# Layer 1's operands between two layers: half the rows transposed by VectorE and moved through DRAM, in a hand-made order

## The chip, the core and the metric

The program runs on one core of one Trainium2 chip. A core has five engines that run side by side and wait for one another on semaphores: TensorE (PE in the profile; its weight loads are PEld), VectorE (DVE), ScalarE (ACT), GpSimd (POOL) and SyncE (SP), which here only issues transfers. The metric is the device time of one execution in microseconds (us), the median of several runs. Positions "at 363.78" are us from the start of the profiled span.

## What is computed

Two layers of attention over 4096 nodes with 512 features; `x` is 4096 x 512 and `adj` 4096 x 4096, both float32. Cut to what matters:

```python
# layer 0: attention inside 32 graphs of 128 nodes each
h = relu(layernorm(x))
x = x + graph_attention(h, adj, adj, ptr, Wq, bq, Wk, bk, Wv, bv)

# layer 1: graph attention over the whole graph, 8 heads of 64
h   = relu(layernorm(x))
mx  = einsum('nf,hfd->hnd', h, W)
t_j = einsum('hnd,hd->hn', mx, a_dst)      # (s_i cancels in the softmax over j)
attn = softmax(where(adj > 0, s_i + t_j, -inf))
x = x + concat_heads(einsum('hij,hjd->hid', attn, mx))
```

In layer 1 the weight of neighbour `j` depends on `j` alone, so the kernel computes `e_j = exp(t_j)` once, multiplies the row `mx_j` by it, and then sums these rows over the neighbours with a 0/1 mask: numerator and denominator come out of one matmul with the mask as the weights. A layer norm of all rows of layer 0's result, a product with `W`, and the scaled rows ("parts") of all 32 row tiles have to stand in SBUF before the first of those sums can end.

## The kernel before

A tile is 128 rows; there are 32 tiles. The steps that the change touches, with cuts marked by `# ...`:

```python
def norm(src, hn):                       # layer norm of a tile
    stats = small.tile([P, 6], F32, name="stats")
    nc.vector.bn_stats(stats, src)                                   # L114
    mv = small.tile([P, 2], F32, name="mv")
    nc.vector.bn_aggr(mv, stats)                                     # L116
    ve = small.tile([P, 1], F32, name="ve")
    nc.gpsimd.tensor_scalar(ve, mv[:, 1:2], EPS, None, ALU.add)      # L118
    rstd = small.tile([P, 1], F32, name="rstd")
    nc.gpsimd.tensor_tensor(rstd, ve, neghalf, ALU.pow)              # L120
    nc.vector.tensor_scalar(hn, src, mv[:, 0:1], rstd, ALU.subtract, ALU.mult)  # L121

def relu_T(ps_pool, hn, dst):            # 4 transposes by TensorE, relu on the way out
    pt = ps_pool.tile([P, KC, P], F32, name="pt")
    for k in range(KC):
        nc.tensor.transpose(pt[:, k, :], hn[:, ts(k, P)], ident)     # L127
    nc.scalar.activation(dst, pt, AF.Relu)                           # L128

def project1(ps_m, hT, w1x):             # product with W, 16 matmuls in the profile
    pm = [ps_m.tile([P, D], F32, name="pp") for _ in range(2)]
    for g, n in ((1, HW + H), (0, HW)):
        for k in range(KC):
            nc.tensor.matmul(pm[g][:, :n], hT[:, k, :], w1x[:, k, g * HW : g * HW + n],
                             start=(k == 0), stop=(k == KC - 1))     # L243
    return pm

def weigh(e, pm):                        # rows times exp(t), two instructions
    for g in (1, 0):
        nc.vector.tensor_tensor(e[:, ts(g, HW)]..., pm[g]..., e[:, ES + ...]..., ALU.mult)  # L252

def split(e, dst):                       # a number as the sum of two fp32r numbers
    nc.scalar.copy(dst[:, :, 0, :], e3)                              # L230
    nc.gpsimd.tensor_sub(dst[:, :, 1, :], e3, dst[:, :, 0, :].bitcast(F32))  # L231

def load_mask(sb, i):                    # 0/1 bytes from DRAM, transposed, cast
    mw = sb.tile([P, P // B, N // BY // (P // B)], F32, name="mw", bufs=1)
    # ... four transfers mw <- a_d (L265)
    nc.vector.transpose(at8..., mw...)                               # L270, 128 x 1024
    at = sb.tile([P, NT, P], F32R, name="at")
    nc.vector.tensor_copy(at..., at8...)                             # L277, 128 x 4096
    return at

def aggregate(sb, ps_g, i, part):        # 32 x 3 matmuls for one tile of the output
    at = load_mask(sb, i)
    pg = ps_g.tile([P, CB, 512], F32, name="pg")
    for j in range(NT):
        for c in range(CB):
            product(pg[:, c], at, part, j, c)                        # L284
    # ...
```

Layer 0 runs first. Behind its last groups, tiles 0 to 8 of layer 1 are begun. Then comes the stretch between the layers, and after it the sums:

```python
def normed1(i):
    row = sb2.tile([P, D], F32, name="row1")
    nc.sync.dma_start(row, x1_d[i])      # layer 0's result, read back from DRAM
    norm(row, row)
    hT = sb2.tile([P, KC, P], F32, name="hT1")
    relu_T(ps_t, row, hT)
    return hT

def prepare(i, hT, part):
    pm = project1(ps_p, hT, w1x)         # ps_p has 4 buffers, a tile takes 2
    e = sb2.tile([P, EW], F32, name="e")
    nc.gpsimd.memset(e[:, EC:], 1.0)
    nc.scalar.activation(e[:, ES:EC], pm[1][:, HW : HW + H], AF.Exp) # L379
    nc.gpsimd.tensor_copy(e_all[:, i, :], e[:, ES:EC])               # L380
    weigh(e, pm)
    split(e, part)
    parts.append(part)

n = len(ahead)                           # 9: tiles 0 to 8 are begun
nhT = ahead[-1]
for i in range(n - 1, NT):
    hT = nhT
    if i + 1 < NT:
        nhT = normed1(i + 1)
    prepare(i, hT, part_tile(lo if i < LO else hi, i))

# ... hold(n, src, bound, op): two DVE instructions that check a range of values

for i in range(NT - 1):
    row = sb3.tile([P, D], F32, name="row3", bufs=1)
    nc.sync.dma_start(row, x1_d[i])
    tot = aggregate(sb3, ps_g, i, lambda j: parts[j])
    # ... divide by the denominator, add row, store
    if i == 1:
        graphs_are_tiles(sb3)            # checks on ptr, small DVE instructions
        hold(0, rs_all, 1.0 / S_MAX, ALU.is_ge)
        # ... three more
```

The order in which an engine gets its instructions is set by a scheduler when the program is built; it may put instructions of the sums (the first masks, the checks) between those of the stretch before. A branch for inputs that break the assumptions ("general") follows and is not taken here.

Of the kernel before, what the change touches and what calls it, by code (L numbers as in the profile page):

```python
# [9 lines left out]
F32 = mybir.dt.float32  # L10
# [10 lines left out]
P = 128  # L21
# [4 lines left out]
H = 8  # L26
# [15 lines left out]
SCALE = float(D) ** -0.5  # L42
BIG_T = 40.0
AB = 7
LO = 8
E_MIN, E_MAX = 4.3e-18, 2.3e17
S_MIN, S_MAX = 1e-15, 1e30
# [4 lines left out]
def kernel(  # L52
# [28 lines left out]

    a_d = dram.tile([NT, P, N // BY], F32, name="a_d")
    x1_d = dram.tile([NT, P, D], F32, name="x1_d")

    ident = const.tile([P, P], F32, name="ident")
# [20 lines left out]
        return a  # L108


    def norm(src, hn):

        stats = small.tile([P, 6], F32, name="stats")
        nc.vector.bn_stats(stats, src)  # L114
# [3 lines that stand above are left out]
        nc.gpsimd.tensor_scalar(ve, mv[:, 1:2], EPS, None, ALU.add)  # L118
        rstd = small.tile([P, 1], F32, name="rstd")
        nc.gpsimd.tensor_tensor(rstd, ve, neghalf, ALU.pow)  # L120
        nc.vector.tensor_scalar(hn, src, mv[:, 0:1], rstd, ALU.subtract, ALU.mult)  # L121

    def relu_T(ps_pool, hn, dst):

# [5 lines that stand above are left out]
    def mask_bytes(a8, a, h):  # L130

        half = ts(h, NW // 2)
        a8v = a8.rearrange("p (u c q b) -> p u c b q", c=NW, q=B, b=BY)[:, :, half]
        av = a.rearrange("p (c b u q) -> p u c b q", c=NW // 2, b=BY, q=B)
        for u in range(P // B):
            nc.vector.tensor_scalar(  # L136
                a8v[:, u], av[:, u], 0.0, None, ALU.is_gt, saturate=False
            )
# [94 lines left out]
    def load_row(pool, i):  # L233
        row = pool.tile([P, D], F32, name="row1")
        nc.sync.dma_start(row, x1_d[ds(i, 1)].rearrange("o p d -> (o p) d"))
        return row

    def project1(ps_m, hT, w1x):
# [4 lines that stand above are left out]
                nc.tensor.matmul(  # L243
                    pm[g][:, :n], hT[:, k, :], w1x[:, k, g * HW : g * HW + n],
                    start=(k == 0), stop=(k == KC - 1),
                )
        return pm

    def weigh(e, pm):

        for g in (1, 0):
            nc.vector.tensor_tensor(  # L252
                e[:, ts(g, HW)].rearrange("p (h d) -> p h d", d=HD),
                pm[g][:, :HW].rearrange("p (h d) -> p h d", d=HD),
                e[:, ES + g * H // 2 : ES + (g + 1) * H // 2, None].to_broadcast([P, H // 2, HD]),
                ALU.mult,
            )
# [48 lines left out]
    def graphs_are_tiles(sb):  # L306


        ptr_i = sb.tile([1, NPTR], I32, name="ptr_i", bufs=1)
        nc.sync.dma_start(ptr_i, ptr)  # L310
        ptr_f = sb.tile([1, NPTR], F32, name="ptr_f", bufs=1)
        nc.vector.tensor_copy(ptr_f, ptr_i)
        ends_i = sb.tile([1, NT, 2], I32, name="ends_i", bufs=1)
        nc.gpsimd.iota(ends_i, pattern=[[P, NT], [P - 1, 2]], base=0, channel_multiplier=0)
        ends = sb.tile([1, NT, 2], F32, name="ends", bufs=1)
        nc.vector.tensor_copy(ends, ends_i)
        ge = sb.tile([1, NT, 2], F32, name="ge", bufs=1)
        for t0 in range(0, NT, 4):
            cmp = sb.tile([1, 8, NPTR], F32, name="cmp", bufs=1)
            nc.vector.tensor_tensor(  # L320
                cmp,
                ends[:, t0 : t0 + 4].rearrange("p t e -> p (t e)")[:, :, None].to_broadcast(
                    [1, 8, NPTR]
                ),
                ptr_f[:, None, :].to_broadcast([1, 8, NPTR]),
                ALU.is_ge,
            )
            nc.vector.tensor_reduce(
                ge[:, t0 : t0 + 4].rearrange("p t e -> p (t e)"), cmp, AX.X, ALU.add
            )  # L330
        same = sb.tile([1, NT], F32, name="same", bufs=1)
        nc.vector.tensor_tensor(same, ge[:, :, 0], ge[:, :, 1], ALU.is_equal)
        later = sb.tile([1, NT - 1], F32, name="later", bufs=1)
        nc.vector.tensor_tensor(later, ge[:, 1:, 0], ge[:, : NT - 1, 1], ALU.is_gt)
        good = sb.tile([1, 2], F32, name="good", bufs=1)
        nc.vector.tensor_reduce(good[:, 0:1], same, AX.X, ALU.min)
        nc.vector.tensor_reduce(good[:, 1:2], later, AX.X, ALU.min)
        nc.vector.tensor_tensor(held[0:1, 6:7], good[:, 0:1], good[:, 1:2], ALU.mult)
# [8 lines left out]
    w1x = None  # L347
    parts = []
    with ExitStack() as straight:
        pool1 = straight.enter_context(tc.tile_pool(name="l1", bufs=1))  # L350
        sb2 = straight.enter_context(tc.tile_pool(name="sb2", bufs=2))
        lo = straight.enter_context(tc.tile_pool(name="lo", bufs=LO // 2))

        with ExitStack() as prep:
            ps_t = prep.enter_context(tc.tile_pool(name="ps_t0", bufs=3, space=PSUM))
            ps_p = prep.enter_context(tc.tile_pool(name="ps_p0", bufs=4, space=PSUM))

            def part_tile(pool, j):
                if j >= LO:
                    return pool.tile([P, CB, 2, CW1], F32R, name=f"part{j}")  # L360
                if j % 2 == 0:
                    two.append(pool.tile([P, 2, CB, 2, CW1], F32R, name=f"part{j}", tag="lo"))
                return two[-1][:, j % 2]
# [3 lines left out]
# [5 lines that stand above are left out]
                relu_T(ps_t, row, hT)  # L372
                return hT

            def prepare(i, hT, part):
                pm = project1(ps_p, hT, w1x)
                e = sb2.tile([P, EW], F32, name="e")
                nc.gpsimd.memset(e[:, EC:], 1.0)
                nc.scalar.activation(e[:, ES:EC], pm[1][:, HW : HW + H], AF.Exp)  # L379
                nc.gpsimd.tensor_copy(e_all[:, i, :], e[:, ES:EC])  # L380
                weigh(e, pm)
                split(e, part)
                parts.append(part)

            with (
                tc.tile_pool(name="w0", bufs=1, side="right") as wp,
                tc.tile_pool(name="adj0", bufs=AB, side="right") as ap,
                tc.tile_pool(name="sb0", bufs=2, side="right") as sb,
                tc.tile_pool(name="ps_s0", bufs=1, space=PSUM) as ps_s,
            ):  # L390
# [178 lines left out]
                        nhT, nr = normed(g + 2)  # L569


            hi = straight.enter_context(
                tc.tile_pool(name="hi", bufs=1, reuse_waits="tile")
            )
            n = len(ahead)
            nhT = ahead[-1]
            for i in range(n - 1, NT):
                hT = nhT
                if i + 1 < NT:
                    nhT = normed1(i + 1)  # L580
                prepare(i, hT, part_tile(lo if i < LO else hi, i))

# [81 lines left out]
    with tc.If(bad > 0, label="general"):  # L666
# [131 lines left out]
        with (  # L798
# [60 lines left out]
            with tc.For_i(0, n_levels, 1):  # L859
                with (  # L860
                    tc.tile_pool(name="sb4", bufs=2) as sb,
                    tc.tile_pool(name="ps_m4", bufs=2, space=PSUM) as ps_m,
                    tc.For_i(0, NT, 1) as i,
                ):
                    hT = sb.tile([P, KC, P], F32, name="hT1")
                    row = load_row(sb, i)
                    norm(row, row)
                    relu_T(ps_t, row, hT)
                    pm = project1(ps_m, hT, w1x)
                    te = small.tile([P, H], F32, name="te")  # L870
                    nc.vector.tensor_tensor(te, pm[1][:, HW : HW + H], shift, ALU.subtract)
                    nc.vector.tensor_scalar(te, te, 0.0, None, ALU.min)
                    e = sb.tile([P, EW], F32, name="e")
                    nc.gpsimd.memset(e[:, EC:], 1.0)
                    nc.scalar.activation(e[:, ES:EC], te, AF.Exp)
                    weigh(e, pm)
                    split(e, parts_e[:, ds(i, 1)].rearrange("p o c s w -> p (o c) s w"))
                with (
                    tc.tile_pool(name="sb5", bufs=1) as sb,
                    tc.tile_pool(name="ps_g5", bufs=1, space=PSUM) as ps_g,  # L880
# [62 lines left out]
```

## Time and profile before

| | |
|---|---|
| time, median of 3 | 964.26 us (963.89 to 967.47) |
| span of the profiled run | 961.1 us |
| TensorE busy | 937.3 us, 98% |
| its weight loads busy | 817.2 us, 85% |
| VectorE, ScalarE, GpSimd busy | 48%, 27%, 19% |
| granted TensorE clock | 0.999 |
| sums of layer 1 (L284, group `pg`) | 479.6 us busy, 3008 matmuls |

How to read it: an engine's busy time is the sum of its instructions; the part of the span that is missing from TensorE's is its idle time. Layer 0 takes the time to about 350, the stretch between the layers goes to about 466, and the sums take the rest. The profile also gives, for any stretch, the busy time of each engine, for each wait who released it, and the instructions in order of time.

### The profile page before, as it was taken

How to read it: one execution, taken by the hardware profiler on the slowest of the kernel's cores; microseconds unless marked ns; L12 is line 12 of the kernel's file. 1: busy time of each engine (PE TensorE's matmuls, PEld its weight loads, DVE VectorE, ACT ScalarE, POOL GpSimd, SP SyncE). 2: the span in 40 equal slices, each digit the busy share in tenths (PEclk: the TensorE clock that was granted, in tenths of full speed). 3: DMA queues.
4: the chain of work that ended last, by engine and by line, in shares of the span. 5: the costliest groups of instructions: out<-in, count | busy, mean ns of one | idle time of the engine just before them, and what ended most of it. 6: DMA issues, size and time to landing. Idle time of an engine off the chain costs nothing.

```text
span 961.1 us, 13194 instructions
## 1 busy us (share of the span) xinstructions
PE 937.3 (98%) x5051; PEld 817.2 (85%) x5051; DVE 460.7 (48%) x983; ACT 260.7 (27%) x507; POOL 185.0 (19%) x344
## 2 busy tenths in 40 slices
PE   8999999989999998899999999999999999999997
PEld 5676677766677776788899999999999999999997
DVE  4678777776766348655142332424233242423322
ACT  5766676666762222333100000000000000000000
POOL 2221213222122115555110101001010100101010
PEclk9999999999999999999999999999999999999999
DMA  9999889898884124222012213132231212122111
GB/s 347 419 349 389 314 324 368 351 369 343 343 335 158 34 87 122 77 66 55 1 54 80 85 49 88 49 83 54 79 82 50 88 50 83 52 80 81 51 45 35
DMA packets 58180, 148.22 MB, mean 154 GB/s; under 512 B 6402, under 2 KB 23170, under 8 KB 49922
## 3 DMA queue, kind: packets, MB, share of 16 engines
q1 hardware_dynamic: 48178, 130.31, 39.0%
q10 hardware_dynamic: 9936, 17.05, 4.7%
q8 instruction: 40, 0.66, 0.3%
q14 instruction: 26, 0.21, 0.1%
HBM read 113.77 MB, written 33.55 MB: 153 GB/s over the span
## 4 chain that ended last, share of the span: by engine, by line
PE 89%; DVE 4%; DMA 2%; POOL 2%; ACT 2%; issue 1%; SPq 0%; ACTq 0%; DVEq 0%; POOLq 0%
PE pg L284 50%; PE pp L428 11%; PE pp L416 10%; PE pp L243 9%; PE pp L501 3%; PE pss L474 3%; PE pt L127 2%; DMA row<-x_d 1%; PE pl L284 1%; POOL part L231 1%; DMA xg<-x 1%; DVE a L136 1%; DVE row L121 1%; ACT junk L451 1%; POOL rstd L120 0%
## 5 line engine op out<-in xcount | busy, mean ns | idle before, releaser
L284 PE MATMUL pg<-part,at 128*128 128x348 f32 x3008 | 479.6, 322 | 1.2 <-DVE e L252 1.2
L284 PEld LDWEIGHTS pg<-part,at 128*128 128x128 f32 x3008 | 479.1, 188 | 1.6 <-issue 1.5
L277 DVE CAST at<-at 128x4096 fp32r<-128x4096 fp8e4 x32 | 74.0, 2313 | 312.2 <-PE pg L284 312.2
L298 ACT COPY tot<-pg 128x522 f32<-128x522 f32 x31 | 18.5, 598 | 455.8 <-PE pg L284 455.8
L451 ACT ACTIVATE junk<-a 128x2048 bf16<-128x2048 f32 (+15 forms) x92 | 124.4, 1353 | 47.1 <-DVE x L503 25.0
L243 PE MATMUL pp<-w1x,hT 128*128 128x256 f32 (+1 forms) x512 | 117.3, 383 | 0.0
L428 PE MATMUL pp<-wv,hT 128*128 128x512 f32 x256 | 114.9, 592 | 0.0
L416 PE MATMUL pp<-hT,m_sb 128*128 128x256 f32 x512 | 113.2, 379 | 0.0
L416 PEld LDWEIGHTS pp<-hT,m_sb 128*128 128x128 f32 x512 | 96.2, 190 | 12.8 <-issue 0.5
L243 PEld LDWEIGHTS pp<-w1x,hT 128*128 128x128 f32 x512 | 94.9, 190 | 13.3
L428 PEld LDWEIGHTS pp<-wv,hT 128*128 128x128 f32 x256 | 48.6, 190 | 60.7 <-issue 60.7
L136 DVE TENSOR_SCALAR a<-a 128x512 fp8e4<-128x512 f32 x256 | 98.1, 460 | 1.8 <-DMA a_d<-a 1.8
L609 POOL COPY den_all<-tot 128x1 f32<-128x1 f32 x31 | 5.7, 184 | 369.2 <-DVE tot L299 369.2
L128 ACT ACTIVATE hT<-pt 128x512 f32<-128x512 f32 x64 | 36.9, 597 | 67.7 <-PE pt L127 67.6
L613 POOL TENSOR_TENSOR tot<-tot,row 128x512 f32<-128x512 f32 x31 | 39.9, 1288 | 61.8 <-DVE tot L304 61.8
L231 POOL TENSOR_TENSOR part<-e,part 128x522 fp32r<-128x522 f32 x32 | 42.2, 1318 | 43.1 <-ACT part L230 35.5
L118 POOL TENSOR_SCALAR ve<-mv 128x1 f32<-128x1 f32 x64 | 18.6, 294 | 150.9 <-DVE mv L116 150.8
L252 DVE TENSOR_TENSOR e<-pp,e 128x256 f32<-128x256 f32 x64 | 26.4, 415 | 29.3 <-ACT e L379 26.0
L270 DVE STREAM_TRANSPOSE at<-mw 128x1024 f32<-128x1024 f32 x32 | 39.6, 1236 | 0.0
L120 POOL TENSOR_TENSOR rstd<-ve,neghalf 128x1 f32<-128x1 f32 x64 | 38.4, 602 | 4.4
L432 DVE TENSOR_TENSOR v<-pp,bv_sb 128x512 f32<-128x512 f32 x32 | 22.0, 688 | 33.9 <-PE pp L428 33.9
L420 ACT ACTIVATE gT<-pp,c_sb 128x256 f32<-128x256 f32 x64 | 29.7, 467 | 28.7 <-PE pp L416 28.3
(101 smaller groups left out, 608.0 us busy)
## 6 DMA issues: line engine op xcount, KB each, us to landing
a<-adj SPq DMA_DIRECT2D x64, 1024.0 KB, 12.9
a_d<-a SPq DMA_DIRECT2D x32, 512.0 KB, 10.2
row<-x_d SPq DMA_DIRECT2D x64, 256.0 KB, 3.4
mw<-a_d SPq DMA_DIRECT2D x128, 128.0 KB, 4.0
xg<-x SPq DMA_DIRECT2D x16, 512.0 KB, 4.6
x_d<-x ACTq DMA_DIRECT2D x32, 256.0 KB, 4.2
out<-tot ACTq DMA_DIRECT2D x31, 256.0 KB, 3.8
wkT_sb<-wkT SPq DMA_DIRECT2D x4, 256.0 KB, 5.0
```

Of the source, the lines that this page charges most:

```text
L120: nc.gpsimd.tensor_tensor(rstd, ve, neghalf, ALU.pow)
L128: nc.scalar.activation(dst, pt, AF.Relu)
L136: nc.vector.tensor_scalar(a8v[:, u], av[:, u], 0.0, None, ALU.is_gt, saturate=False)
L231: nc.gpsimd.tensor_sub(dst[:, :, 1, :], e3, dst[:, :, 0, :].bitcast(F32))
L243: nc.tensor.matmul(pm[g][:, :n], hT[:, k, :], w1x[:, k, g * HW : g * HW + n], start=(k == 0), stop=(k == KC - 1),)
L270: nc.vector.transpose(at8.rearrange("p c n b -> p (c n b)").bitcast(F32).rearrange("p (c u n) -> p c u n", c=NW, n=B), mw.rearrange("p u ( ...
L277: nc.vector.tensor_copy(at.rearrange("p (c b) q -> p c b q", b=BY), at8.rearrange("p c q b -> p c b q"))
L284: nc.tensor.matmul(pg[:, : 2 * CW1], at[:, j, :], part(j)[:, c].rearrange("p s w -> p (s w)"), start=(j == 0), stop=(j == NT - 1),)
L416: nc.tensor.matmul(pp[:, : G * P], m_sb[:, k, ts(m, P)], hT[:, k, :], start=(k == 0), stop=(k == KC - 1),)
L428: nc.tensor.matmul(pp, hT[:, k, ts(t, P)], wv[:, k, :], start=(k == 0), stop=(k == KC - 1))
L451: nc.scalar.activation(junk[:, c0:c1], a[:, c0:c1], AF.Exp, scale=2.0 * NEG, accum_out=sums[:, n : n + 1],)
L613: nc.gpsimd.tensor_add(num, num, row)
```

## The change

Tiles 16 to 31 of layer 1 no longer go through TensorE's transposes. VectorE normalises the rows, ScalarE applies the relu, VectorE transposes 32 x 32 blocks, and four such tiles (a "block" of 1 MB) are stored to a DRAM tensor and loaded again so that the blocks land in the places of a whole transpose. The rows within a group of four tiles come out in another order; the mask's bytes of the second half of the columns are put into the same order, so that the sum is the same. Tiles 9 to 15 stay with TensorE. VectorE, ScalarE, GpSimd and SyncE keep the order in which the loop is written, 8 tiles ahead for the new kind of tile and 2 tiles ahead for the old kind. The pools of the stretch move to the other side of SBUF and end with it; the small `ptr` load shares a buffer with `row3`.

```diff
+MIXED = NT // 2
+AHEAD = 8
+    hT_d = dram.tile([NW, P, P // B, KC * P], F32, name="hT_d")
-    def norm(src, hn):
+    def moments(src):                       # the first four instructions of norm
...
+        return mv[:, 0:1], rstd
+    def norm(src, hn, of=None):
+        mean, rstd = of or moments(src)
+        nc.vector.tensor_scalar(hn, src, mean, rstd, ALU.subtract, ALU.mult)
...
-        av = a.rearrange("p (c b u q) -> p u c b q", c=NW // 2, b=BY, q=B)
+        order = ("p (c b u q) -> p u c b q", "p (c u b q) -> p u c b q")[h]
+        av = a.rearrange(order, c=NW // 2, b=BY, q=B)
...
-        ptr_i = sb.tile([1, NPTR], I32, name="ptr_i", bufs=1)
+        ptr_i = sb.tile([1, NPTR], I32, name="ptr_i", tag="row3", bufs=1)
...
-        pool1 = straight.enter_context(tc.tile_pool(name="l1", bufs=1))
-        sb2 = straight.enter_context(tc.tile_pool(name="sb2", bufs=2))
+            pool1 = prep.enter_context(tc.tile_pool(name="l1", bufs=1, side="right"))
+            sb2 = prep.enter_context(tc.tile_pool(name="sb2", bufs=2, side="right"))
...
-            for i in range(n - 1, NT):
-                hT = nhT
-                if i + 1 < NT:
-                    nhT = normed1(i + 1)
-                prepare(i, hT, part_tile(lo if i < LO else hi, i))
+            def load(i):
+                if i < NT:
+                    name, bufs = ("rowm", 5) if i >= MIXED else ("rown", 3)
+                    rows[i] = sb4.tile([P, D], F32, name=name, bufs=bufs)
+                    nc.sync.dma_start(rows[i], x1_d[i])
+            def turn(i):
+                c, b = divmod(i, BY)
+                if b == 0:
+                    blocks[c] = sb4.tile([P, P // B, KC, BY, B], F32, name="blocks")
+                nc.vector.transpose(
+                    blocks[c][:, :, :, b], rows[i].rearrange("p (k q f) -> p q k f", k=KC, f=B)
+                )
+                if b == BY - 1:
+                    nc.sync.dma_start(hT_d[c], blocks[c].rearrange("p q k b r -> p q (k b r)"))
+            def move(c):
+                hT = sb5.tile([P, P // B, KC, P], F32, name="hT4")
+                for q in range(P // B):
+                    nc.sync.dma_start(
+                        hT[ts(q, B)].rearrange("p u k m -> p u (k m)"),
+                        hT_d[c, :, q].rearrange("(u f) w -> f u w", f=B),
+                    )
+                for u in range(BY):
+                    hTs[c * BY + u] = hT[:, u]
+            with tc.manual_schedule(engines={E.DVE, E.Activation, E.Pool, E.SP}):
+                n = len(ahead) - 1                                  # 8
+                hTs[n] = ahead[n]
+                before = None
+                for i in (1, 2):
+                    load(n + i)
+                for i in range(MIXED, n + AHEAD + 2):
+                    load(i)
+                norm(rows[n + 1], rows[n + 1])
+                for i in range(n, NT):
+                    far, near = i + AHEAD, i + 2
+                    near_in = near < MIXED
+                    far_in = MIXED <= far < NT
+                    if near + 1 < MIXED:
+                        load(near + 1)
+                    load(far + 2)
+                    if MIXED <= far - 1 < NT:
+                        turn(far - 1)
+                    if (far - 2) % BY == BY - 1 and MIXED <= far - 2 < NT:
+                        move((far - 2) // BY)
+                    if far_in:
+                        of[far] = moments(rows[far])
+                    if near_in:
+                        of[near] = moments(rows[near])
+                    if i + 1 < MIXED:
+                        hTs[i + 1] = sb2.tile([P, KC, P], F32, name="hT1")
+                        relu_T(ps_t, rows[i + 1], hTs[i + 1])
+                    pm = project1(ps_p, hTs[i], w1x)
+                    if before:
+                        finish(*before)                             # weigh, split of tile i - 1
+                    if near_in:
+                        norm(rows[near], rows[near], of[near])
+                    if far_in:
+                        norm(rows[far], rows[far], of[far])
+                    before = (weights(i, pm), pm, part_tile(lo if i < LO else hi, i))
+                    if far_in:
+                        nc.scalar.activation(rows[far], rows[far], AF.Relu)
+                finish(*before)
```

`weights` and `finish` are the two halves of `prepare`. The rest of the diff is in the branch that is not taken.

## The prediction

> **What bounds the kernel now.** The first view is the page: the span and TensorE's busy share.
>
> ```profile
> span 961.1 us, 13194 instructions
> PE 937.3 (98%) x5051; PEld 817.2 (85%) x5051; DVE 460.7 (48%) x983; ACT 260.7 (27%) x507; POOL 185.0 (19%) x344
> ```
>
> TensorE is the bound: all its idle time together is 961.1 - 937.3 = 23.8 us. A change can win only by taking work from TensorE or by closing some of these gaps. The second view is busy time by stretch (columns: length, then busy us of each engine):
>
> ```profile
> 356.00:404.00 48.00, 41.83 (x203) 34.23 (x202) 38.98 (x79) 13.02 (x29) 25.98 (x49) 1.00 0.34 98
> 404.00:457.00 53.00, 53.00 (x270) 46.07 (x269) 29.34 (x66) 16.95 (x40) 30.31 (x68) 1.00 0.23 61
> 457.00:466.00 9.00, 7.83 (x39) 6.58 (x37) 3.46 (x9) 2.53 (x6) 2.82 (x5) 1.00 0.00 0
> ```
>
> Between the layers TensorE has 48.00 - 41.83 = 6.17 us of gaps while VectorE is loaded (38.98 of 48), then none for 53 us, then 1.17 us at the handover to the sums. The third view, TensorE's waits, says who ends them: mainly VectorE's normalised rows.
>
> ```profile
> PE pt L127 <- DVE row L121: 8.7, 5, 3.0
> PE pg L284 <- DVE e L252: 1.2, 1, 1.2
> ```
>
> The fourth, the chain in order of time, gives the steady tile: 3.51 us of product and 0.44 us of transposes, with nothing between.
>
> ```profile
> 437.69 3.51 PE pp L243 x16
> 441.20 0.44 PE pt L127 x4
> 441.63 3.51 PE pp L243 x16
> ```
>
> [...] a row normalisation at 375.39 took 1.44 us in place of 0.55 while GpSimd's subtraction (L231, from 375.32, 1.23 us) ran. [...]The page's row loads of 256 KB land in 3.4 us and pairs of 512 KB in 4.6[...].
>
> **Part 1: removed from TensorE.** 16 tiles x 0.44 us = 7.0 us of transposes, all on the path. ScalarE's copy out of PSUM (L128, 597 ns) goes too, and a relu of about the same size comes instead.
>
> **Part 2: the 6.2 us of gaps now.** They come because the scheduler put three masks (L270 1.24 + L277 2.3 us each) and the small ptr checks between the norms. By the built program's order these now all stand after the stretch. So these gaps go, if VectorE's new work doesn't make others.
>
> **Part 3: VectorE's new loop.** While both kinds of tile are in work (tiles 8 to 13) one turn of the loop is, in order, with start-to-start times as the trace has them where VectorE is packed: transpose 0.6 (half of L270's 1.24), twice stats and aggregate 0.83, two products with e 0.75, a wait of 0.25 (in the steady timeline a norm starts 1.0 us after its aggregate has ended, which is GpSimd's L118 and L120; the products hide 0.75 of it), two norms 0.5 each. That is 4.3 us. Then the last norm feeds ScalarE's relu and the relu feeds the next turn's first transpose: 0.1 + 0.6 + 0.1 = 0.8 us in which VectorE has nothing to do. 5.1 us a turn, against TensorE's 3.95. Walking the first turns from tile 8's product, at about 362.9 (363.78 now, less the 0.4 and 0.5 of gaps before it): VectorE is ahead by about one turn, so TensorE first waits at tile 11, 0.5 us, and then 1.25 or 1.3 at tiles 12, 13 and 14: 4.3 us together. With the far kind alone (tiles 14 to 23) a turn is 0.6 + 0.83 + 0.75 + 0.25 + 0.5 + 0.8 = 3.75 to 3.85 against 3.51: TensorE has only 2 x 2 PSUM buffers and follows, 8 x 0.33 = 2.6 us. After tile 23 VectorE has only the products and TensorE runs at 3.51.
>
> **Part 4: the trip through DRAM.** Four tiles make a store of 1 MB and four loads of 256 KB. The only 1 MB transfers of this kind that land while not queued by their own kind took 6.8 and 7.5 us; the loads need four issues at 0.45 us, and the last should land in some 4.5 us (the mask quarters of 128 KB on 32 partitions took 4.0). About 13 us from the block's last transpose to the product. The walk gives 16 us for the first block, 13.2 for the second and third, and 11.8 for the last, whose lead shrinks because TensorE no longer waits for VectorE. I count 1.3 us for the last and nothing for the others.
>
> **Part 5: the handover.** The built program has the first mask's transpose after the last product of VectorE's loop and after the range checks. The order now is shown by the timeline: checks in front of the last L252, the sums right after it, with their mask long ready.
>
> ```profile
> 463.60 0.29 DVE L595 TENSOR_SCALAR ok<-e_all 128x256 f32<-128x256 f32 x1 [0.16 <-POOL e_all L380]
> 463.93 0.42 DVE L596 TENSOR_REDUCE held<-ok 128x1 f32<-128x256 f32 x1
> 464.38 0.29 DVE L595 TENSOR_SCALAR ok<-e_all 128x256 f32<-128x256 f32 x1
> 464.71 0.42 DVE L596 TENSOR_REDUCE held<-ok 128x1 f32<-128x256 f32 x1
> 465.04 0.41 DVE L252 TENSOR_TENSOR e<-pp,e 128x256 f32<-128x256 f32 x1
> 465.60 20.63 PE L284 MATMUL pg<-part,at 128*128 128x348 f32 x128 [1.17 <-DVE e L252]
> ```
>
> After the change TensorE has to wait for: the last L252, 0.45; nine small checks, about 2.3 (the four of e_all above take 1.5); L270 1.2; L277 2.3; a start of 0.1. That is 6.4 us, against 1.17 now.
>
> **The sum.** From 362.9: 24 products x 3.51 = 84.2; 6 transposes left x 0.44 = 2.6; VectorE's turns 4.3 + 2.6; the last block 1.3; the handover 6.4. The sums start at 464.3, against 465.60 now: 1.3 us earlier. The 496 us after that hold the same matmuls in the same order; the ptr checks that move there (eight pairs of 0.83 us) fit in a tile's 15.5 us. Layer 0's matmuls keep their order. 964.26 - 1.3 = 963.0.
>
> **The rivals.** (a) *VectorE doesn't bind.* If the order of the loop leaves VectorE ahead, the 6.9 us of part 3 are gone, and the time is about 956. For it: far rows are taken 8 tiles ahead, and only the near norms and the PSUM buffers tie the two engines. Against it: the relu between two instructions of the same in-order engine, with nothing of VectorE's placed between. (b) *The DRAM trip binds.* If store and loads take 16 us in place of 13, three blocks stall 3 us each: about 971. For it: the loads write 32 partitions at a time and SyncE, in order, holds the row loads behind the wait for the store. Against it: transfers are light here (a busy share of 0.23 and 0.34 in the stretches above) and the first block has 3 us to spare. (c) [...] In turns with two norms the second comes about when GpSimd's subtraction starts, which can hold it 0.9 us as at 375.39; five times that is 4.5 us: about 967. (d) *Handover hidden.* Nothing I see hides it; if it were hidden, 5 us less.
>
> **Range and chances.** The sum lies near zero because a sure 7.0 + 6.2 us is set against 6.9 + 1.3 + 5.2 us whose first two terms are rough. (a) and (d) pull down by 5 to 7, (b) and (c) up by 4 to 8. I take 963.0, with 955 to 971. 2% is 19.3 us: more than all transposes and gaps of this stretch together (14.4), so a gain of that size has no source; a loss of that size needs the DRAM trip to be twice as slow. Faster by 2%: 0.01; within: 0.96; slower: 0.03.
>
> **What would show each step right or wrong.** In the profile after: L127's matmuls on rows fall by 64; the gap before the first sum is 6 to 7 us and is ended by the cast of the mask, not by L252 (part 5); small gaps of about 1.3 us before the transposes of tiles 12 to 14, released by VectorE's norm, and VectorE idle 0.8 us before each block transpose, released by ScalarE's relu (part 3); from tile 16 on, products 3.8 us apart with no transposes between, waiting for L252; no wait for the loads of hT4 but before the last block (part 4). It would be wrong above all if products waited several us for hT4 at every fourth tile, or if no wait for VectorE were left at all.

## The result, and the profile after

The changed kernel takes 970.21 us (median of 6 runs, 968.94 to 971.12) beside 964.08 us for the kernel before (median of 6): ratio 1.0054, 95% interval 1.0037 to 1.007. It is slower by 5 to 6 us (the medians differ by 6.1, the means, 970.06 and 964.87, by 5.2, which is the ratio given); the prediction was 1.3 us less than before.

The same views, of the changed kernel. First the page:

```profile
span 968.4 us, 13109 instructions
PE 936.7 (97%) x4987; PEld 813.1 (84%) x4987; DVE 470.6 (49%) x999; ACT 260.5 (27%) x507; POOL 176.3 (18%) x344
```

64 matmuls fewer (x4987 against x5051), as planned, and TensorE's busy time is still nearly that of before. Its idle time is 968.4 - 936.7 = 31.7 us, against 23.8. The busy time by stretch (columns: length, busy us of PE, PEld, DVE, ACT, POOL with instructions, then the granted clock, the DMA share and GB/s) says where:

```profile
356.00:404.00 48.00, 42.70 (x201) 34.46 (x200) 31.66 (x63) 16.28 (x37) 23.43 (x51) 1.00 0.41 121
404.00:457.00 53.00, 52.40 (x233) 43.24 (x233) 28.02 (x64) 16.54 (x39) 28.42 (x64) 1.00 0.60 159
457.00:470.00 13.00, 4.33 (x21) 3.46 (x19) 6.88 (x14) 1.43 (x3) 2.85 (x5) 0.82 0.09 24
...
470.00:473.00 3.00, 3.00 (x10) 3.00 (x11) 0.91 (x1) 0.00 (x0) 0.00 (x0) 0.50 0.26 72
473.00:476.00 3.00, 3.00 (x13) 3.00 (x13) 2.63 (x2) 0.00 (x0) 0.00 (x0) 0.55 0.42 129
476.00:479.00 3.00, 3.00 (x21) 3.00 (x20) 1.25 (x1) 0.00 (x0) 0.00 (x0) 1.00 0.17 45
```

Between the layers there are still 5.3 us of gaps (48.00 - 42.70). Before the sums, 8.67 of 13 us are idle. And the first six microseconds of the sums do half the matmuls (10 and 13 in 3 us, against 21): the clock reads 0.50 and 0.55 there. TensorE's waits (us in total, times, longest):

```profile
PE pg L294 <- DVE at L287: 8.7, 1, 8.7
PE pt L136 <- DVE rown L130: 4.4, 4, 1.9
...
PE pt L136 <- DVE row L130: 2.8, 1, 2.8
...
PE pp L253 <- DVE e L262: 0.9, 2, 0.6
PE pp L253 <- DMA hT<-hT_d: 0.4, 1, 0.4
```

The largest is the handover: the first sum waits for the cast of its mask, where it waited 1.2 us for the last product with e before.

The two profiles add up. Positions are those of tile 8's product, of the end of the last product and of the first sum, in us:

| | before | after | difference |
|---|---|---|---|
| layer 0 and tiles 5 to 7: to tile 8's product | 363.78 | 365.17 | +1.4 |
| tile 8's product to the end of the last product | 100.65 | 96.15 | -4.5 |
| idle before the first sum | 1.17 | 8.67 | +7.5 |
| the sums, to the end of the span | 495.5 | 498.4 | +2.9 |
| span | 961.1 | 968.4 | +7.3 |

In the first row two things meet. Tile 7's product starts at 358.37 before and at 360.37 after, and these 2.0 us are not the change's. Most of them arise near 216 us, where both kernels wait for a row's norm (2.54 us before, 2.80 after): the clock (third from the right) then fell in the profile of after and not in that of before. Before:

```profile
215.00:220.00 5.00, 3.66 (x10) 1.80 (x11) 2.87 (x7) 3.93 (x10) 0.91 (x3) 1.00 1.04 437
```

and after:

```profile
215.00:220.00 5.00, 3.55 (x6) 1.78 (x7) 1.67 (x4) 2.91 (x8) 1.02 (x3) 0.66 1.03 433
```

From tile 7's product to tile 8's the change gains 0.6 us (5.41 before, 4.80 after), since a wait there is gone. The profile of before, with a granted clock of 0.999, was a lucky one: of 78 further runs of that kernel 7 had 0.999 (mean 963.2 us), 25 had 0.997 (965.1) and 26 had 0.995 (966.4). So about 2 of the 7.3 us are in the choice of the profile.

### The profile page after: what moved, and what is told of

It is laid out like the page before. It is cut to its first block, busy times and chain, and to the rows that moved or that the text cites. A ratio compares the mean times of both kernels' runs of the same rounds, so it can differ in the third digit from the quotient of the medians.

```text
span 968.4 us, 13109 instructions
## 1 busy us (share of the span) xinstructions
PE 936.7 (97%) x4987; PEld 813.1 (84%) x4987; DVE 470.6 (49%) x999; ACT 260.5 (27%) x507; POOL 176.3 (18%) x344
## 4 chain that ended last, share of the span: by engine, by line
PE 84%; DMA 5%; DVE 5%; ACT 2%; POOL 2%; issue 1%; SPq 0%; ACTq 0%; POOLq 0%; DVEq 0%
PE pg L294 50%; PE pp L444 10%; PE pp L432 9%; PE pp L253 7%; PE pp L517 3%; PE pss L490 2%; DMA a<-adj 2%; DMA row<-x_d 1%; PE pt L136 1%; POOL rstd L124 1%; PE pl L294 1%; DVE stats L118 1%; DVE a L146 1%; DVE rowm L130 1%; ACT junk L467 1%
## 5 line engine op out<-in xcount | busy, mean ns | idle before, releaser
L241 POOL TENSOR_TENSOR part<-e,part 128x522 fp32r<-128x522 f32 x32 | 40.2, 1255 | 40.6 <-ACT part L240 30.9
L122 POOL TENSOR_SCALAR ve<-mv 128x1 f32<-128x1 f32 x64 | 16.3, 258 | 161.8 <-DVE mv L120 161.8
L517 PE MATMUL pp<-v,sT 128*128 128x512 f32 x64 | 34.6, 623 | 2.8 <-ACT sT L511 2.4
```

Source lines behind the costliest of these rows:

```text
L517: nc.tensor.matmul(po, sT[:, t, :], v, start=True, stop=True)
```

## Experiments

All ratios are to the kernel before, run on the same chip in the same series (which chip the changed kernel ran on is not known). The series used three chips, so the difference of two ratios carries both intervals. "Stretch" is from tile 8's product to the end of the last product, "gap" the idle time before the first sum, "sums" the rest of the span, all from the profiles, in us.

| kernel | ratio (95%) | stretch | gap | sums |
|---|---|---|---|---|
| before | 1 | 100.65 | 1.17 | 495.5 |
| changed | 1.0054 (1.0037 to 1.007) | 96.15 | 8.67 | 498.4 |
| hand order alone | 1.0020 (1.0012 to 1.0029) | 93.99 | 8.66 | 498.3 |
| trip through DRAM alone | 1.0043 (1.0030 to 1.0055) | 95.97 | 8.67 | 498.6 |
| checks later | 0.9982 (0.9975 to 0.9989) | 96.05 | 4.81 | 498.0 |
| TensorE kept at work, first try | 1.0172 (1.0155 to 1.0189) | 96.25 | 6.28, after 13.9 of extra work | 497.9 |
| TensorE kept at work, second try | 1.0022 (1.0014 to 1.0030) | 96.21 | 0.52 + 1.02 | 496.3 |
| early mask | 0.9950 (0.9928 to 0.9972) | 96.40 | 2.00 | 496.4 |
| early mask, transposes behind the statistics | 0.9866 (0.9840 to 0.9893) | 86.96 | 1.96 | 496.6 |
| the same, nine tiles ahead | 0.9872 (0.9844 to 0.9901) | 86.96 | 1.99 | 496.3 |
| early mask, transposes two turns behind | 0.9884 (0.9857 to 0.9911) | 88.53 | 1.96 | 495.8 |
| early mask, hand order, no trip | 0.9929 (0.9906 to 0.9951) | 93.98 | 2.00 | 496.0 |
| all together, and rows loaded earlier in layer 0 | 0.9817 (0.9795 to 0.9838) | 86.96 | 0.61 | 495.8 |

**The hand order alone.** All rows through TensorE again, the loop's order kept.

```diff
-MIXED = NT // 2
+MIXED = NT            # no tile of the new kind; the mask's bytes in their old order
```

> The hand-made order kept, the trip through DRAM taken out: all rows of layer 1 are transposed by TensorE again (0.44 us a tile). My theory: a VectorE turn is then statistics 0.83, products 0.74, one norm 0.5, far below TensorE's 3.95 us a tile, so no gap is left between the layers; tiles 8 to 31 take 24 x 3.95 = 94.8 us in place of the 96.15 of the changed kernel, and the handover gap of 8.7 us and the low clock after it stay as they are, since the first mask still stands behind everything: about 969 us, 1.3 less than the changed kernel. Rival: the gain between the layers comes from the DRAM route, and the order alone keeps the gaps of before (100.65 us for this stretch): about 975.

Ratio 1.0020. As my theory had it: no gap is left between the layers, and the stretch is 93.99. That is 6.7 us better than before without any trip, and 2.2 us better than with it. The trip saved TensorE 7.0 us of transposes and brought back 9.2 us of waits. This kernel keeps the order, norms two tiles ahead in place of one, and no masks between them; which of these closes the gaps was not tried.

**The trip alone.** The scheduler orders the engines.

```diff
-            with tc.manual_schedule(engines={E.DVE, E.Activation, E.Pool, E.SP}):
+            if True:
```

> The trip through DRAM kept, the hand-made order taken out: the scheduler orders VectorE, ScalarE, GpSimd and the loads. My theory: the order matters, because VectorE's turn is about as long as TensorE's; the scheduler's order puts transposes and norms ahead of products that free PSUM, so TensorE waits more: tiles 8 to 31 take 2 to 6 us longer than the 96.15 of the changed kernel, total 972 to 976. The handover is the same in this order (checks, then mask), 8 to 9 us. Rival: the order is of no weight, only the route: within 1 us of the changed kernel's 970.2.

Ratio 1.0043, stretch 95.97: my theory was wrong and the rival right. The scheduler's order is as good as the hand-made one as it stands. It has other waits (3.6 us for products with e, 2.6 for ScalarE's hT, only 0.4 for VectorE's row norm), which add up to the same. And its handover is the same 8.67 us, as it is 8.66 without the trip, so that gap comes neither from the hand-made order nor from the trip. What both keep is the change's new place for the pools: the first mask's buffer lies where those of the stretch were. That this is what keeps the mask back is likely, but was not tried by itself.

**The checks later.** The range checks and GpSimd's ramp behind the second tile of the sums.

```diff
-        nc.gpsimd.memset(held, 1.0)
             if i == 1:
+                nc.vector.tensor_tensor(held, num[:, :7], num[:, :7], ALU.is_equal)   # waits for tile 1
                 graphs_are_tiles(sb3)        # ends_i and ok now share row3's buffer
```

> The changed kernel with the range checks (and the index ramp from GpSimd that VectorE waits 2.2 us for) moved behind the second tile of the sums, where VectorE has room; the first mask is then straight behind the last product with e. My theory: the gap before the sums falls from 8.67 to 0.45 + 1.23 + 2.29 + 0.15 = 4.1 us, so 4.5 us less. The clock: 2.54 us of idleness kept it in layer 0 of the kernel before and 2.8 us lost it in the changed kernel, so 4.1 us still loses it, and the sums stay at about 498.4: in all about 965.7. Rival: how much clock is lost goes with the length of the idle time: then half of the 2.9 us comes back too, about 964.3. Second rival: the checks, now among the sums, delay a mask by more than they saved: 968 or more.

Ratio 0.9982, 6.9 us less than the changed kernel by the ratios, of which about 2 are uncertain by the intervals; the medians differ by 5.2 (965.04 and 970.21). The gap is 4.81, not 4.1, because the cast, now earlier, meets GpSimd's subtraction and takes 3.01 us in place of 2.29 (VectorE in order of time; columns: start, duration):

```profile
461.68 1.24 DVE L280 STREAM_TRANSPOSE at<-mw 128x1024 f32<-128x1024 f32 x1
462.95 3.01 DVE L287 CAST at<-at 128x4096 fp32r<-128x4096 fp8e4 x1
```

The clock falls after this gap too (0.51 from 467 to 470), and the sums take 498.0: of the 2.9 us only 0.4 came back. The profiles explain 3.9 us in the gap and 0.4 in the sums; the rest is left open. In the series of the changed kernel the kernel before had a median of 964.08, in this one 966.16, and such a difference goes into the ratios.

**TensorE kept at work, first try.** Matmuls without use in the gap.

```diff
                 finish(*before)
+                for _ in range(4):
+                    pt = ps_t.tile([P, KC, P], F32, name="pt")
+                    for k in range(KC):
+                        nc.tensor.matmul(pt..., hTs[NT - 1][:, k, :], w1x[:, k, :D], start=(k == 0), stop=(k == KC - 1))
```

> The changed kernel with 16 matmuls of 128 x 512 more (about 7.0 us) on TensorE between the last product of layer 1 and the first sum, where it idles 8.7 us; their result is not used. My theory: the sums take 498.4 us in place of 495.5 because the idle TensorE lost its granted clock (0.50 to 0.74 from 464 to 476 us). Kept at work it keeps the clock: the first sum starts where it did (about 470.0), the clock reads 1.00 in 470 to 476, the sums take 495.5 us, and the time falls by 2.9 to about 967.3. Rival: the sums are longer for another reason (the checks that moved into them, masks that come late): then the time stays at 970.2, or grows if the matmuls get in the way.

Ratio 1.0172, 11 us more than the changed kernel: it failed as an experiment in two ways. A matmul of 128 x 512 takes 0.87 us here and not the half that I took, so the sixteen took 13.9 (the profile lists two matmuls for each one of the program, hence x32). And they read `hT4` and `w1x`, whose memory the checks and masks of the sums use next, so VectorE began on them only when the last matmul was done (busy 0.00 us from 464 to 476, 1.57 from 476 to 479; TensorE in order of time):

```profile
463.16 13.90 PE L669 MATMUL pt<-w1x,hT 128*128 128x512 f32 x32
483.34 16.95 PE L294 MATMUL pg<-part,at 128*128 128x348 f32 x91 [6.28 <-DVE at L287]
```

After those 6.28 us of idleness the clock had fallen again (0.70 from 479 to 485, 0.89 from 485 to 500, and 1.00 from 461 to 479 while the extra matmuls ran).

**TensorE kept at work, second try.** Half as many, on data that no later buffer waits for.

```diff
+                for _ in range(2):
+                    pt = ps_t.tile([P, KC, P], F32, name="pt")
+                    for k in range(4):
+                        nc.tensor.matmul(pt..., ident, before[0][:, :D], start=(k == 0), stop=(k == 3))
```

> Eight matmuls of 128 x 512 (0.88 us each by the sixteen of the run before, 7.0 us in all) on TensorE in the changed kernel's handover gap, this time on data that no mask or check has to wait for (the last tile's e and the identity); their result is not used. My theory, the lost clock: they fill about 461.8 to 468.9, the first sum still starts near 470, the granted clock reads 1.00 in 470 to 476 in place of 0.50 to 0.55, the sums take 495.5 us in place of 498.4, and the time falls by 2.9, to a ratio of about 1.0025 to the kernel before. Rival: the sums are longer for another reason (checks that moved into them, masks that come late): then nothing changes, ratio 1.0054.

Ratio 1.0022, as expected (1.0025). The first sum is at 468.99, 8.68 us after the last product as in the changed kernel, and the clock (third from the right) stays:

```profile
470.00:473.00 3.00, 3.00 (x21) 3.00 (x20) 1.95 (x2) 0.00 (x0) 0.00 (x0) 1.00 0.00 0
473.00:476.00 3.00, 3.00 (x21) 3.00 (x20) 1.59 (x1) 0.00 (x0) 0.00 (x0) 1.00 0.61 180
```

Doing useless work saves 3.1 us by the ratios (with an uncertainty of nearly 2 by the intervals); the sums take 496.3 in place of 498.4, the checks and masks in them being those of the changed kernel. So of the 2.9 us in the sums 2.1 are the lost clock. Where the other 0.8 are is open: every later kernel that keeps the clock at 1.00 into the sums takes 495.8 to 496.6 for them, with the handover changed or not.

**The early mask.** As the checks later, and the first mask's transpose and cast ahead of the last tile's two products with e.

```diff
+                way.close()                        # the pools of rows and blocks end here
+                sb3 = straight.enter_context(tc.tile_pool(name="sb3", ..., reuse_waits="tile"))
+                at_0 = load_mask(sb3, 0)           # in the memory of rows and blocks, free by now
                 finish(*before)
```

> As the run with the later checks, and the first mask's transpose and cast stand in VectorE's order one product with e before the last one (its buffer lies where the rows of layer 1 were, so it is free by then); 3.5 us of VectorE beside a product of 3.51. My theory: the gap before the sums falls from 8.67 to about 1 us (the last e and the start, as in the kernel before), the clock stays at 1.00, the sums take 495.5: 7.6 + 2.9 = 10.5 us less than the changed kernel, ratio about 0.994 to 0.995. Rival: the mask's work delays the last product with e, and the gap is still 3 to 4 us and costs the clock: ratio about 0.998, as with the later checks alone.

Ratio 0.9950, 10.0 us less than the changed kernel (expected 10.5). The gap is 2.00, not 1.0: the cast takes 3.05 us beside GpSimd (2.29 alone) and holds the last products with e back by about a microsecond. The clock stays at 1.00, the sums take 496.4.

**The transposes behind the statistics.** With the early mask, one move in VectorE's loop:

```diff
-                    if MIXED <= far - 1 < NT:
-                        turn(far - 1)
                     if far_in:
                         of[far] = moments(rows[far])
                     if near_in:
                         of[near] = moments(rows[near])
+                    if MIXED <= far - 1 < NT:
+                        turn(far - 1)
```

> As the run before, and in VectorE's loop the block transpose stands behind the statistics in place of ahead of them, so that the relu it waits for (0.7 us in each turn) runs beside the statistics. My theory: the turn falls from 5.1 to 6.0 us to 4.1 to 5.0 with both kinds of tile and from 3.75 to about 2.8 with the far kind alone, so TensorE's pace of 3.51 to 3.95 binds: the waits for VectorE's row norm fall from 4.4 to under 2.5 us, and those of the far turns (2.6) go; a transpose that comes 1.5 us later in its turn and a shorter turn leave the trip through DRAM less time, 1 to 2.5 us of new waits for its loads at three blocks. From tile 8's product to the end of the last product 92 us in place of 96.15; in all 3 to 5 us less than the run before. Rival: VectorE's norms held by GpSimd's subtraction set the pace, not the relu: then no change.

Ratio 0.9866, 8.1 us less than with the early mask alone, more than the 3 to 5 expected. One turn of VectorE in the changed kernel:

```profile
388.35 0.55 DVE L130 TENSOR_SCALAR rown<-rown,mv,rstd 128x512 f32<-128x512 f32 x1 [0.42 <-POOL rstd L124]
388.81 1.49 DVE L130 TENSOR_SCALAR rowm<-rowm,mv,rstd 128x512 f32<-128x512 f32 x1
391.00 0.71 DVE L611 STREAM_TRANSPOSE blocks<-rowm 128x512 f32<-128x512 f32 x1 [0.69 <-ACT rowm L664]
...
394.35 0.55 DVE L130 TENSOR_SCALAR rown<-rown,mv,rstd 128x512 f32<-128x512 f32 x1 [0.41 <-POOL rstd L124]
```

and with the transposes moved:

```profile
377.46 0.55 DVE L130 TENSOR_SCALAR rown<-rown,mv,rstd 128x512 f32<-128x512 f32 x1 [0.15 <-POOL rstd L124]
377.92 0.54 DVE L130 TENSOR_SCALAR rowm<-rowm,mv,rstd 128x512 f32<-128x512 f32 x1
...
379.99 0.68 DVE L612 STREAM_TRANSPOSE blocks<-rowm 128x512 f32<-128x512 f32 x1
...
381.56 0.55 DVE L130 TENSOR_SCALAR rown<-rown,mv,rstd 128x512 f32<-128x512 f32 x1 [0.24 <-POOL rstd L124]
```

From near norm to near norm 6.00 us became 4.10: in these turns the wait for the relu is gone, part of that for GpSimd's rstd, and the second norm takes 0.54 and not 1.49: it now begins ahead of GpSimd's subtraction (at 378.41), where in the changed kernel it began behind it (388.81 after 388.75). TensorE has no wait at all left between 354 and 451 us. The stretch is 86.96, and 24 products at 3.51 with 6 transposes at 0.44 are 86.9. The new waits for the trip's loads that I expected do not appear.

**Nine tiles ahead.** One turn more for the trip.

```diff
-AHEAD = 8
+AHEAD = 9            # and row 16 is normalised before the loop
```

> As the run before, and the far rows are taken nine tiles ahead in place of eight: one turn more (3.5 us) for the trip through DRAM. My theory: no wait for its loads is left, and TensorE goes through tiles 8 to 31 in 24 x 3.51 + 6 x 0.44 = 87 us and some 1 to 2 us of waits for VectorE at tiles 11 to 14: 88 to 89 us in place of 96.15, 2 to 4 us less than the run before, ratio about 0.987 to the kernel before. Rival: the trip isn't what TensorE waits for; then the time is that of the run before.

Ratio 0.9872, stretch 86.96: no change, the rival. There was nothing left to win: the trip was not what TensorE waited for.

**The transposes two turns behind.** With the early mask, the transpose ahead of the statistics as in the change, but of the row before.

```diff
-                        turn(far - 1)
+                        turn(far - 2)        # and move() one turn later
```

> The changed kernel with the early mask, and its block transpose taken two turns after the norm in place of one, at the same place of VectorE's turn (ahead of the statistics): this takes away the wait for the relu (0.70 us a turn) and leaves the order of norms and products. It tells apart the two things that went with the transpose's move behind the statistics: the relu, and the norm that takes 1.4 us in place of 0.55 beside GpSimd's subtraction. If the norm still meets the subtraction: a mixed turn is 0.63 + 1.58 + 0.74 + 0.38 + 0.5 + 1.4 = 5.2 us against 3.95, the waits for VectorE's row norm fall from 4.5 to 2 or 3 us, the far turns (3.05) no longer bind, and tiles 8 to 31 take 90 to 91 us (96.4 before, 86.96 at best). If the meeting goes too, 87 to 88. The trip through DRAM has a turn less of lead (3.5 us): where that binds, 1 to 3 us come on top, seen as waits for hT. Ratio about 0.990.

Ratio 0.9884, stretch 88.53. No wait for VectorE is left; one wait of 1.21 us for the trip's loads is, at 397.24, ahead of tile 16, the first block: with a turn less of lead the trip binds there, and only there. Taking the relu's wait away was enough here to end the waits for VectorE: of the five turns with both kinds, four had a slow second norm (1.46 to 1.50 us) in the changed kernel; two still have one here (1.49 and 1.46), and TensorE waits for neither, because VectorE is ahead. So the relu in VectorE's path was needed for the waits. The meetings with GpSimd made the turns longer, but were not tried by themselves, and two of the four went away together with the relu's wait here.

**Early mask and hand order, no trip.** The first experiment's edit with the early mask's.

```diff
-MIXED = NT // 2
+MIXED = NT
+                at_0 = load_mask(sb3, 0)           # ahead of the last tile's products with e, as above
```

> The hand-made order with the early mask and without the trip through DRAM: beside the kernel with trip, early mask and moved transposes (ratio 0.9866) it tells what the trip is worth when nothing waits. My theory: 16 tiles' transposes, 7.0 us: tiles 8 to 31 take 93.9 in place of 86.96, ratio about 0.994, the same as with the trip as the change has it (0.995). Rival: the trip also frees TensorE in other ways, or costs in others, and the two differ by less than 5 or more than 9 us.

Ratio 0.9929, stretch 93.98, as expected. Beside it, the kernel with the trip and the moved transposes has 86.96: the trip is worth 7.0 us of the stretch, all that was promised, once nothing waits (6.1 us by the ratios). As the change has it, the trip is worth less than nothing: 1.0054 with it and 1.0020 without. With the early mask the stretch says the same (96.40 and 93.98), while the intervals of the two ratios (0.9950 and 0.9929) overlap.

**All together.** The transposes behind the statistics, the first mask ahead of the last two tiles' products with e, and in layer 0 each row loaded one step earlier.

```diff
                             ahead.append(normed1(i))
+                            fetch(i + 1)              # its load, one step ahead
```

> The trip through DRAM with the transposes behind the statistics, the first mask two products with e before the last, and in layer 0 each row of layer 1 loaded one step earlier than it is normalised, so that TensorE does not wait 2.5 us for the third row near 213 us, a wait after which the clock was low in five of nine traces so far. My theory: that wait goes (2.5 us) and with it the lost clock (1.5 to 2 us in the traces that show it), and the handover gap falls from 2.0 to 1.2: 3.5 to 5 us less than with the transposes moved alone (952.3 on its chip), ratio 0.982. Rival: the row arrives early, but TensorE then waits for ScalarE's or VectorE's work in the same place: ratio 0.986, as before.

Ratio 0.9817, 947.88 us beside 965.90 for the kernel before on that chip: faster than both kernels. The wait near 216 us is gone with its lost clock (1.00 from 213 to 225), and the gap is 0.61. At 215.60 TensorE now waits 1.60 us for ScalarE (4.0 us in all for `sT`, against 2.4), so a part of the rival holds too. Its waits:

```profile
PE pp L524 <- ACT sT L518: 4.0, 5, 1.6
...
PE pg L294 <- POOL e_all L396: 0.6, 1, 0.6
```

## Why the prediction was right or wrong, by its own steps

The number fell into the range, near its upper end, but the sign was wrong. That it fell inside is partly luck: the upper end stood for a DRAM trip that binds (b), which did not come, or for meetings of the second norm with GpSimd's subtraction (c), which did, while two causes of the miss, the ramp in the handover and the lost clock, were in no rival.

- **Part 1, transposes off TensorE, 7.0 us: right.** The runs with and without the trip, with nothing waiting, differ by 93.98 - 86.96 = 7.0 us.
- **Part 2, the gaps of 6.2 us go: right.** The hand order alone has none of them, and gains 6.7 us in the stretch.
- **Part 3, VectorE's loop, 4.3 + 2.6 us: the mechanism right, the size too small.** The stretch is 96.15 against 86.9 without waits; less 0.4 for the loads, VectorE cost 8.9 us, not 6.9. The mis-sized term is the 4.3 us of the turns with both kinds. From tile 8's product to tile 14's (365.17 to 395.44) TensorE took 30.3 us, where six tiles at 3.95 are 23.7: 6.6 us. A turn was predicted at 5.1 us; from near norm to near norm three of four took 6.0, with a second norm of 1.49 or 1.50 us that began 0.01 to 0.06 us behind GpSimd's subtraction, and the one whose second norm took 0.54, begun 0.21 us ahead of the subtraction, took 5.06. That was rival (c), put beside the sum and not into it. The far turns came as predicted: 3.75 us from norm to norm.

VectorE in a far turn of the changed kernel:

```profile
425.69 0.55 DVE L130 TENSOR_SCALAR rowm<-rowm,mv,rstd 128x512 f32<-128x512 f32 x1 [0.36 <-POOL rstd L124]
426.94 0.71 DVE L611 STREAM_TRANSPOSE blocks<-rowm 128x512 f32<-128x512 f32 x1 [0.70 <-ACT rowm L664]
...
429.44 0.55 DVE L130 TENSOR_SCALAR rowm<-rowm,mv,rstd 128x512 f32<-128x512 f32 x1 [0.36 <-POOL rstd L124]
```

The idle 0.70 ended by ScalarE's relu is the one that the prediction named. TensorE's share of it is not listed as waits: its 233 matmuls from 404 to 457 would take 51.1 us at the 3.51 for 16 of the steady tile, and are shown as 52.40 us busy.

- **Part 4, the trip, 1.3 us for the last block: nearly right.** One wait of 0.36 us, at 418.02, and not before the last block. Rival (b) didn't come; a turn more of lead gains nothing, a turn less costs 1.2. One size was too high: the store of 1 MB landed in 3.9 to 4.5 us, not in the 6.8 to 7.5 taken from other transfers; the loads took 4.0 to 6.5, where 4.5 was taken.
- **Part 5, the handover, 6.4 us: the mechanism right, a term left out.** The gap is ended by the mask's cast, as predicted, but it is 8.67. The page of work in order of time shows the missing term:

```profile
461.35 0.42 DVE L262 TENSOR_TENSOR e<-pp,e 128x256 f32<-128x256 f32 x1 [1.02 <-PE pp L253]
...
462.59 1.23 POOL L241 TENSOR_TENSOR part<-e,part 128x522 fp32r<-128x522 f32 x1 [2.11 <-ACT part L240]
463.77 0.27 POOL L324 IOTA ends_i<- 1x64 int32 x1
464.07 0.18 DVE L326 CAST ends<-ends_i 1x64 f32<-1x64 int32 x1 [2.21 <-POOL ends_i L324]
...
466.27 1.23 DVE L280 STREAM_TRANSPOSE at<-mw 128x1024 f32<-128x1024 f32 x1
467.54 2.29 DVE L287 CAST at<-at 128x4096 fp32r<-128x4096 fp8e4 x1
469.98 3.24 PE L294 MATMUL pg<-part,at 128*128 128x348 f32 x10 [8.67 <-DVE at L287]
```

One of the nine small checks takes GpSimd's ramp, and GpSimd is at its last subtraction: VectorE stands still for 2.21 us with the mask behind it. I counted the checks' durations and not what they wait for.

- **"The sums after that unchanged": wrong.** They took 2.9 us longer. What the prediction did not think of is that this gap of 8.67 us on TensorE is paid twice. The second try to keep it at work shows it: first sum 8.68 us after the last product, clock at 1.00, 2.1 us less in the sums.
- **"Layer 0 unchanged": right of the work, not of the profile.** Its clock fell in this profile; that it does so in most runs of the kernel before too is suggested by their granted clocks, but no trace of them shows it.

The differences of the terms give the miss in the spans: layer 0's clock and the start of tile 8 2.3 (362.9 predicted, 365.17; 2.0 of it layer 0, and 0.3 because the prediction took 0.9 us of gaps ahead of tile 8, where the change gained 0.6), the stretch 1.1 (95.0 predicted), the handover 2.3, the sums 2.9; together 8.6, which is +7.3 against -1.3.

## What to carry to other kernels

In a loop whose order is kept as written, look at where an engine's own result comes back to it through another engine: placed behind work that was ready anyway, that trip (0.69 us of VectorE's idleness in a turn) was no longer waited for, and moving one instruction was worth 8.1 us here, more than the 7.0 us of transposes that the change removed. When a change moves the work between two phases, walk the first instruction of the next phase back through each engine's order, with every wait and not only the durations on the way. Gaps on TensorE from 2.40 us on could cost the clock too here, so close them, or fill them, before counting smaller things.

## What the runs showed of the hardware that was not expected

**The clock.** After idle gaps of 4.81 us (checks later) and of 8.66 to 8.67 (changed, hand order alone, trip alone) the granted clock read 0.50 or 0.51. By readings over 3 us it came back 4 to 6 us after the matmuls had begun again (in the changed kernel they begin at 469.98, and the clock reads 0.55 for 473 to 476 and 1.00 from there). After 6.28 us (first try to keep TensorE at work) it read 0.70 from 479 to 485 and 0.89 from 485 to 500. The sums took 497.9 to 498.6 us after these gaps, and 495.8 to 496.6 in the later kernels that kept the clock; my estimate from these is about 2 us each time. After the shorter gap of 4.81 us it was back sooner, at 470 with the matmuls begun at 466.11, but the sums took only 0.4 us less than in the changed kernel. After gaps of 1.96 to 2.00 us at the same place it stayed at 1.00, in five profiles. In between no sharp limit was seen: near 216 us gaps of 2.54, 2.58, 2.64 and 2.88 us kept the clock, and gaps of 2.40, 2.41, 2.47, 2.48, 2.62, 2.80, 2.87 and 2.92 lost it (lowest readings 0.50 to 0.80); in the kernel before a gap of 3.02 us, ended at 376.88, kept it (1.00 from 370 to 384). So in these profiles the length of a gap alone did not decide; what did was not found.

**VectorE beside GpSimd.** VectorE's cast of a mask takes 2.29 us alone and 3.01 or 3.05 beside GpSimd, and GpSimd can lose time too: in the kernel with the early mask its copy of 128 x 8 numbers, 0.19 us in the median, took 2.25 while that cast ran.

```profile
457.81 1.23 POOL L241 TENSOR_TENSOR part<-e,part 128x522 fp32r<-128x522 f32 x1 [2.11 <-ACT part L240]
458.17 3.05 DVE L287 CAST at<-at 128x4096 fp32r<-128x4096 fp8e4 x1
...
459.01 2.25 POOL L389 COPY e_all<-e 128x8 f32<-128x8 f32 x1
```

GpSimd's subtraction began first and kept its 1.23 us; the cast, which began in the middle of it, took 0.76 longer; the copy began at 459.01 and ended at 461.26, just after the cast (461.22). Why the two engines slow each other is not shown by these runs. Not every instruction of VectorE was slower beside GpSimd's subtraction: with the transposes moved, the statistics fall beside its subtraction (from 374.27, 1.29 us), and take 0.69 and 0.66 us, where the changed kernel has 0.65 and 0.66.
